# First attention layer: the weighting of the values cut into column halves beside light work, and the transposed maxima moved one step later into another bank ring

## The chip, the cores and the metric

The kernel runs on one core of a Trainium2 chip. The metric is the device time of one execution in microseconds (us); the times of a kernel are given as the median over several runs. Besides these there is one profiled execution, whose instruction records the profile is made of. Engines are named as in the profile: PE is the matrix engine, PEld its weight loads, DVE the vector engine, ACT the scalar engine, POOL the general-purpose engine, SP the one that issues most DMAs.

## The reference, cut to what matters

The model is two layers of attention, each with two attention blocks and a feed-forward block, on x of 2 x 512 rows of 512 numbers. The change is inside the first block, a latent attention with 32 heads, a query latent of 12 and a key latent of 4:

```python
C_q = x @ Wq_d + bq_d
C_kv = x @ Wkv_d + bkv_d
q = (C_q @ W_qk + b_qk).reshape(b, s, NUM_HEADS, KV_LAT)
scores = jnp.einsum('bqhd,bkd->bhqk', q, C_kv) / jnp.sqrt(jnp.asarray(KV_LAT, x.dtype))
attn = jax.nn.softmax(scores, axis=-1)
V = (C_kv @ Wv_u + bv_u).reshape(b, s, NUM_HEADS, HEAD_DIM)
out = jnp.einsum('bhqk,bkhd->bqhd', attn, V).reshape(b, s, NUM_HEADS * HEAD_DIM)
return out @ Wo + bo
```

There is no mask, so every one of 512 queries sees 512 keys. Since the values are an up-projection of a latent of 4, the kernel weights the latent itself (4 numbers and a one, which sums the weights) and applies a folded product of the up-projection and `Wo` afterwards.

## The kernel before

`attn_latent_small` holds all eight PSUM banks. Four heads make a quartet; 32 heads in 2 batches are 16 quartets, called units u = 0 to 15 here. A unit has these operations, each on a tile of 128 by 512:

- `score` (L589, reduce at L597): 16 products of 128 queries by 512 keys, four heads g on four row groups of 32 rows of PE. DVE takes the row maximum of each. The results rotate through a ring of three banks, kind "S" (banks 0 to 2).
- `split` (L606, L607) on POOL, then `maxima` (L615, L199, L618): four PE transposes of the maxima, one correcting product, and an ACT copy into `qm`, the queries with their maxima folded in. Before the change the result lies in an "S" bank.
- `transposed` (L627, L630): the scores again, keys down and queries across, and their exponents by ACT into `pt` or `room`. The results rotate through a ring of three banks, kind "T" (banks 3 to 5).
- `values` (L637): for one key tile, four products with 32 columns of weights each (one for each head, side by side in the columns of PE), over 512 queries, summed in bank 6 over the 4 key tiles and the 4 quartets of a half.

The order of PE is written out by hand; the other engines' order follows from a scheduler. The loop takes eight steps for a unit. Every step issues two scores (of a unit 12 steps ahead), then two transposed scores, which use the two row groups that the two scores leave free. After them an even step issues `values` of a key tile that is two tiles behind, and an odd step a piece of other work (`slices`): a chained product L473, a `head` projection L503 with its ACT copy L513 and its POOL pair L481 and L482, a `divide`, a product L686 or L903, a layer norm's transposes L228, or an `add`, which is a POOL addition L248 and nothing on PE. Step 6 has `maxima` of the next unit between the transposed scores and `values`. The `qm` that it makes is first read by `transposed` in step 0 of the next unit.

So a step is one burst of four row-group products followed by one larger piece, and PE takes its work strictly in this order: a product whose bank is not yet free holds back all that follows. A "S" bank is freed by DVE's reduce, a "T" bank by ACT's exponent (or by the copy to `qm`).

Other engines' orders that matter: DVE runs the reduces of L597 in order with small work of the pieces (L525 and L560 for example), ACT the exponents in order with the copies of the pieces.

Of the kernel before, what the change touches and what calls it, by code (L numbers as in the profile page):

```python
# [38 lines left out]
B, S, D = 2, 512, 512  # L39
P = 128  # L40
NT = S // P
KC = D // P
NTILES = B * NT
# [385 lines left out]
def attn_latent_small(k, a):  # L429
# [9 lines left out]
    with ExitStack() as ctx:  # L439
# [31 lines left out]
        def chained(ps, pairs):  # L471
            for i, (lhsT, rhs) in enumerate(pairs):
                nc.tensor.matmul(ps, lhsT, rhs, start=(i == 0), stop=(i == len(pairs) - 1))  # L473
                yield 1

        def halved(engine, out, full, at, tag="high"):

            top = lp.tile(list(out.shape), F32R, tag=tag, name="high")  # L480
            engine.tensor_scalar(top, full, low[:, at : at + 1], 1.0, ALU.mult, ALU.mult)  # L481
            return engine.tensor_tensor(out, full, top.bitcast(F32), ALU.add).ins  # L482
# [3 lines left out]
        def latents(b):  # L486
            ps = k.turn()
            yield from chained(ps, [(wkvd[:, c], k.xT[b][:, c]) for c in range(KC)])
            full = fulls[b] = one([P, S], "full")
            nc.vector.tensor_scalar(full, ps, bkvc, None, ALU.add)  # L490
            k.latest = halved(nc.gpsimd if b else nc.vector, keys[b], full, 0)

        def queries(b):
            ps = k.turn()
            yield from chained(ps, [(wqd[:, c], k.xT[b][:, c]) for c in range(KC)])
            full = one([P, S], "full")
            nc.vector.tensor_scalar(full, ps, bqd, 0.5, ALU.add, ALU.mult)
            cqs[b] = one([P, S], "cq", F32R)
            halved(nc.gpsimd if b else nc.vector, cqs[b], full, 2)

        def head(b, t):
            ps = k.turn()
            nc.tensor.matmul(ps, wqks[:, t], cqs[b], start=True, stop=True)  # L503
            if (b, t) < (0, 2):
                top = lp.tile([P, S], F32R, tag="high", name="high")
                nc.scalar.copy(top, ps)
                yield 1
                k.correct(ps, rest, top)
                nc.scalar.copy(qs[b][:, t], ps)
                yield 0  # L510
                return
            full = one([P, S], "wv_diag")
            nc.scalar.copy(full, ps)  # L513
            halved(nc.gpsimd, qs[b][:, t], full, 1)
            yield 1

        def latent_values(b):

            tp = k.turn()
            for t in range(NT):  # L520
                nc.tensor.transpose(tp[:, bass.ts(t, P)], fulls[b][:, bass.ts(t, P)], k.ident)
            part = tp.rearrange("p (t d) -> p t d", t=NT)[:, :, 0:5]
            for i in range(4):
                to = vals[b][:, :, i, 5 * i : 5 * i + 5]
                k.latest = nc.vector.tensor_copy(to, part).ins  # L525
            yield 1
# [12 lines left out]
        def fold():  # L539

            wv_diag = one([P, KC, H, 4], "wv_diag")
            nc.vector.tensor_tensor(
                wv_diag,
                own.unsqueeze(3).broadcast_to([P, KC, H, 4]),
                wvT.unsqueeze(2).broadcast_to([P, KC, H, 4]),
                ALU.mult,
            )
            yield 0
            ps = k.turn()
            yield from chained(  # L550
                ps, [(wv_diag[:, c].rearrange("p h d -> p (h d)"), wo[:, c]) for c in range(KC)]
            )
            nc.scalar.copy(folded, ps)
# [3 lines left out]
        def fold_bias():  # L557

            bv_rep = one([P, KC, P], "wv_diag")
            nc.vector.tensor_copy(bv_rep, bvu.unsqueeze(2).broadcast_to([P, KC, P]))  # L560
            yield 0
            ps = k.turn()
            yield from chained(ps, [(bv_rep[:, c], wo[:, c]) for c in range(KC)])
            bias = one([P, D], "bias_all")
            nc.vector.tensor_tensor(bias, ps, bo, ALU.add)
            added.append(bias)

        def add(t):
            with tc.issue_after(k.pooled):
                k.add_bias(t, added[0])  # L570
            yield 1

        quartets = [(b, half, i) for b in range(B) for half in range(2) for i in range(4)]
        last = len(quartets) - 1
        qm, probs, raws, ctxs = {}, {}, {}, {}
# [4 lines left out]
        of_values, other = 6, (7,)  # L580

        def own_bank(kind):
            turns[kind] = (turns[kind] + 1) % 3
            return k.held[:, banks[kind][turns[kind]]]
# [16 lines left out]
        def split(u):  # L601


            every = nm[u % 2].rearrange("p t (g e) -> p t g e", g=4)
            top = lp.tile([P, NT, 4], F32R, tag="top", name="top")
            nc.gpsimd.tensor_copy(top, every[:, :, :, HIGH])  # L606
            k.pooled = nc.gpsimd.tensor_tensor(  # L607
                every[:, :, :, LOW], every[:, :, :, HIGH], top.bitcast(F32), ALU.subtract
            ).ins

        def maxima(u):
            b, half, i = quartets[u]
            tp = own_bank("S")
            for qt in range(NT):
                nc.tensor.transpose(tp[:, bass.ts(qt, P)], nm[u % 2][:, qt], k.ident)  # L615
            k.correct(tp, unit, qs[b][:, 4 * half + i])
            t = lp.tile([P, S], F32R, tag="qm", name="qm")
            nc.scalar.copy(t, tp)  # L618
            qm[u] = t
# [9 lines left out]
            )  # L629
            nc.scalar.activation(probs[u, kc][:, g], ps, AF.Exp)  # L630

        def values(u, kc):
            b, half, i = quartets[u]
            acc = k.held[:, of_values]
            pt = probs.pop((u, kc))
            for g in range(4):
                nc.tensor.matmul(  # L637
                    acc[rows[g]],
                    vals[b][:, kc, i],
                    pt[:, g],  # L640
                    start=(i == 0 and kc == 0),
                    stop=(i == 3 and kc == NT - 1),
                )
            if i == 3 and kc == NT - 1:
                raws[u] = one([P, S], "raw")
                nc.scalar.copy(raws[u], acc)
                extra.extend(following(u))
# [91 lines left out]
        def next_scores():  # L739
            at = next(scores, None)  # L740
            if at:
                u, qt, p = at
                for g in (2 * p, 2 * p + 1):
                    score(u, qt, g)
                if (qt, p) == (NT - 1, 1):
                    split(u)
# [47 lines left out]
        extra = [centre(NT, NT + 1), head(0, 2), head(0, 3), put(NT), put(NT + 1)]  # L794
        extra += [centre(NT + 2, NT + 3), latent_values(0), head(0, 4), put(NT + 2)]
        extra += [put(NT + 3), head(0, 5), head(0, 6), head(0, 7)]

        later = [queries(1), latents(1)] + [head(1, t) for t in range(4)] + [latent_values(1)]
        later += [fold_bias()] + [head(1, t) for t in range(4, 8)] + [fold()]
        later += [add(t) for t in range(NTILES)]  # L800

        behind = []
        with tc.manual_schedule(engines={mybir.EngineType.PE}):
            for n in range(12):
                next_scores()
                slices(1)
                fill(2, of_values)
                if n == 7:
                    with tc.issue_after(k.latest):
                        adapter_coefficients(k, a)  # L810
                if n == 8:
                    maxima(0)
            run(extra)
            extra = later
            k.ring = other
            for u in range(len(quartets)):
                if u == last:
                    k.ring = (0, 1, 2, 7)
                for step in range(8):
                    next_scores()  # L820
                    for g in (2, 3) if step % 2 == 0 else (0, 1):
                        transposed(u, step // 2, g)
                    if step == 6 and u < last:
                        maxima(u + 1)
                    if step % 2 == 0 and len(behind) > 1:
                        values(*behind.pop(0))
                        if u == last:
                            slices(1)
                    else:
                        slices(2 if u == last else 1)  # L830
                    if step % 2:
                        behind.append((u, step // 2))
            k.ring = (0, 1, 2, 3, 4, 5, 7)
            for at in behind:
                values(*at)
            run(extra)
# [1518 lines left out]
```

## Time and profile before

| | us |
|---|---|
| median of 3 runs | 1966.57 (1964.31 to 1967.5) |
| the profiled execution's own time | 1969.02 |
| its span, first to last instruction | 1967.3 |
| the stage of the first attention's 16 units | about 42 to 255 of the span |
| PE busy in the span | 1929.8 (98%) |
| DVE, ACT, POOL busy | 1372.4, 937.8, 1019.7 |

The times of the stage below are read from the timeline (instructions in order of time, one engine at a time) and from busy times of chosen stretches. In a timeline line the first number is the start, the second the length; a run of records is merged, with its count after "x", and what the engine waited for just before stands in brackets. Starts are in us from the start of the span. A matmul in 32-bit floats without the rounded type has two records.

### The profile page before, as it was taken

What the parts mean: (1) busy time and instruction counts of PE and PEld (TensorE: products, weight loads), DVE (VectorE), ACT (ScalarE), POOL (GpSimd) and SP (SyncE); (2) the same over time, 40 slices, a digit from 0 to 9 for tenths busy, and PEclk for the clock granted to TensorE, in tenths of its full rate; (3) what the DMA queues carried; (4) which work ended last, traced back from release to release, by engine and by line L of the source; (5) the groups of instructions that cost most, each with busy time, mean ns of one, the idle gap of its engine ahead of it and who ended that gap; (6) DMA issues with size and microseconds to landing.
All of it is one profiled execution on the core that took longest, in us unless ns stands there. A gap on an engine that the chain in (4) does not pass through costs nothing.

```text
span 1967.3 us, 40475 instructions
## 1 busy us (share of the span) xinstructions
PE 1929.8 (98%) x15610; PEld 1195.7 (61%) x15610; DVE 1372.4 (70%) x3457; ACT 937.8 (48%) x2460; POOL 1019.7 (52%) x1112
## 2 busy tenths in 40 slices
PE   9989999999999999999999999999999999999999
PEld 5333356777777777777777545666566554654554
DVE  8889658767776676777765577777677755847853
ACT  3876624444444343444443267666666411641550
POOL 4331055776756667677763246565655545216221
PEclk9999999999999999999999999999999999999999
DMA  3010222322321322232222213020101002002001
GB/s 136 17 44 1 75 68 65 90 73 88 98 65 50 97 76 81 76 98 76 79 79 85 71 22 109 7 74 7 62 13 55 25 9 49 2 2 43 2 2 43
DMA packets 69296, 108.96 MB, mean 55 GB/s; under 512 B 13922, under 2 KB 48994, under 8 KB 62052
## 3 DMA queue, kind: packets, MB, share of 16 engines
q1 hardware_dynamic: 68804, 104.15, 18.2%
q8 instruction: 127, 2.08, 0.4%
q0 software_dynamic: 288, 2.10, 0.3%
q14 instruction: 77, 0.63, 0.1%
HBM read 80.00 MB, written 4.19 MB: 43 GB/s over the span
## 4 chain that ended last, share of the span: by engine, by line
PE 87%; DVE 5%; POOL 5%; issue 1%; ACT 1%; DMA 0%; SPq 0%; DVEq 0%; POOLq 0%
PE held L1004 13%; PE held L281 11%; PE held L1139 9%; PE held L190 9%; PE held L357 8%; PE held L637 3%; PE held L589 3%; PE held L1076 3%; PE held L473 2%; PE sc L190 2%; PE held L1498 2%; PE held L1495 1%; PE pj L190 1%; PE tp L1771 1%; PE held L1496 1%
## 5 line engine op out<-in xcount | busy, mean ns | idle before, releaser
L302 ACT ACTIVATE room<-room,nmax 128x128 f32<-128x128 f32 (+3 forms) x384 | 212.6, 557 | 354.4 <-DVE nmax L292 352.0
L281 PE MATMUL held<-kT,q 128*32 128x32 f32 (+15 forms) x4096 | 264.2, 397 | 5.3 <-DVE invs L310 1.7
L292 DVE CUSTOM_DVE_ANT_0 room<-held,mask 128x128 f32<-128x128 f32 (+3 forms) x384 | 179.1, 488 | 62.5 <-PE held L281 57.0
L281 PEld LDWEIGHTS held<-kT,q 128*32 128x32 f32 x4096 | 143.4, 110 | 87.2 <-issue 37.7
L357 PE MATMUL held<-turned,vals 32*128 32x384 f32 (+7 forms) x2784 | 189.7, 416 | 0.9 <-issue 0.9
L597 DVE TENSOR_REDUCE nm<-held 128x1 f32<-128x512 f32 x256 | 161.7, 684 | 23.4 <-PE held L627 14.6
L357 PEld LDWEIGHTS held<-turned,vals 32*128 32x128 f32 (+1 forms) x2784 | 149.3, 167 | 39.8 <-issue 23.2
L315 ACT ACTIVATE room<-room,invs 128x128 f32<-128x128 f32 (+3 forms) x316 | 153.3, 551 | 41.8 <-DVE invs L310 41.7
L254 DVE TENSOR_TENSOR rows<-rows,held 128x512 f32<-128x512 f32 x198 | 129.5, 673 | 31.9 <-PE held L1004 31.3
L330 DVE STREAM_TRANSPOSE turned<-room 128x1152 f32<-128x1152 f32 x80 | 107.9, 1361 | 41.2 <-ACT room L315 21.6
L243 POOL TENSOR_TENSOR rstd<-ve,mhalf 128x1 f32<-128x1 f32 x64 | 36.2, 569 | 179.5 <-DVE ve L241 176.3
L1165 POOL TENSOR_TENSOR q<-q,room 128x256 f32<-128x256 f32 x64 | 45.3, 729 | 123.4 <-DVE q L1148 112.8
L1183 POOL TENSOR_TENSOR q<-q,cosq 128x512 f32<-128x512 f32 x60 | 88.0, 1467 | 31.6 <-DVE t L1180 31.6
L1139 PE MATMUL held<-room,w 128*128 128x256 f32 x384 | 95.0, 383 | 0.0
L1184 POOL TENSOR_TENSOR q<-q,t 128x512 f32<-128x512 f32 x64 | 86.8, 1356 | 6.3 <-DVE q L1183 2.5
L302 ACT ACTIVATE probs<-probs,nmax 128x128 f32<-128x128 f32 (+3 forms) x128 | 70.6, 553 | 37.8 <-DVE nmax L292 37.0
L589 PEld LDWEIGHTS held<-keys,qs 32*128 32x128 f32 x256 | 30.9, 181 | 94.2 <-DVE nm L597 67.5
L1004 PE MATMUL held<-w,ctxT 128*128 128x256 f32 x360 | 86.5, 383 | 0.1
L630 ACT ACTIVATE pt<-held 128x512 f32<-128x512 f32 x128 | 69.7, 598 | 29.8 <-PE held L627 24.9
L630 ACT ACTIVATE room<-held 128x512 f32<-128x512 f32 x128 | 69.8, 599 | 26.7 <-PE held L627 25.0
L589 PE MATMUL held<-keys,qs 32*128 32x512 f32 x256 | 76.9, 494 | 5.5 <-DVE nm L597 5.1
L2105 POOL TENSOR_SCALAR_AFFINE_SELECT room<-room 128x512 f32<-128x512 f32 x32 | 20.3, 635 | 118.0 <-ACT room L2101 118.0
(439 smaller groups left out, 5011.0 us busy)
## 6 DMA issues: line engine op xcount, KB each, us to landing
w<-in_b_wq SPq DMA_DIRECT2D x16, 1024.0 KB, 4.8
w<-in_b_wo SPq DMA_DIRECT2D x16, 1024.0 KB, 5.2
vals<-v SPq DMA_DIRECT2D x256, 64.0 KB, 2.1
w<-in_m_wo SPq DMA_DIRECT2D x8, 1024.0 KB, 6.7
w<-in_b_wk SPq DMA_DIRECT2D x16, 256.0 KB, 2.8
w<-in_b_wupv SPq DMA_DIRECT2D x16, 256.0 KB, 2.6
w<-in_m_wqn SPq DMA_DIRECT2D x8, 384.0 KB, 3.4
rows<-in_x SPq DMA_DIRECT2D x8, 256.0 KB, 4.7
```

The costliest lines, as they stand in the source:

```text
L190: last = self.nc.tensor.matmul(out, lhsT, rhs, start=(i == 0), stop=(i == len(pairs) - 1))
L254: self.nc.vector.tensor_tensor(x, x, ps.rearrange("p (t d) -> p t d", t=2), op)
L281: nc.tensor.matmul(ps[32 * i : 32 * i + 32, a - lo : b - lo], q[:, at : at + 32], keys[:, a:b], start=True, stop=True,)
L292: nc.vector.tensor_tensor_reduce(out=row, in0=ps[:, :kv], in1=self.mask_back[:, :kv] if qt % 2 else self.mask[:, S - kv :], op0=ALU.add, o ...
L302: nc.scalar.activation(row, row, AF.Exp, bias=nmax, scale=-1.0, accum_out=total[:, qt : qt + 1])
L315: self.nc.scalar.activation(row, row, AF.Identity, scale=each)
L357: self.nc.tensor.matmul(out[:, :, :n], values(i, j), rhs, start=(j == blocks[0]), stop=(j == stop[i]),)
L589: nc.tensor.matmul(ps, qs[b][rows[g], 4 * half + i, bass.ts(qt, P)], keys[b][rows[g]], start=True, stop=True,)
L597: k.latest = nc.vector.tensor_reduce(nm[u % 2][:, qt, at : at + 1], ps, AX.X, ALU.max, negate=True).ins
L630: nc.scalar.activation(probs[u, kc][:, g], ps, AF.Exp)
L1004: k.nc.tensor.matmul(out, lhsT[:, i, bass.ts(t, P)], rhs[i], start=not (after or t or i), stop=i == 1, skip_group_check=True,)
L1139: nc.tensor.matmul(out, lhsT[:, c], rhs[:, c], start=c == 0, stop=c == 1)
```

## The change

It does two things, both in the order of PE.

- `maxima` of the next unit moves from step 6, where it stood behind the transposed scores, to step 7, where it stands between the two scores and the two transposed scores; and it takes its bank from the "T" ring instead of the "S" ring.
- `values` can be told to do a part of the columns. Where the next piece of other work is a `head` or an `add`, or there is none, a step 0, 2 or 4 issues only columns 0 to 255 of the four products, and the next odd step issues columns 256 to 511 ahead of its piece. The first and last tile of a sum are excepted. Laid out, this happens for 10 tiles: three of unit 2 (steps 0, 2, 4), one of unit 4 (step 0) and three each of units 6 and 7; 80 matmuls of 256 columns stand where 40 of 512 stood.

ACT, POOL and SP keep their orders. DVE's order differs in a few places: in unit 2 the copy L560 goes ahead of the copies L525 and of the reduces of step 6, in unit 4 the multiplication L542 goes behind the reduces of step 7, and in one place of the second batch two layer-norm operations change places with two reduces.

```diff
         def maxima(u):
             b, half, i = quartets[u]
-            tp = own_bank("S")
+            tp = own_bank("T")
...
-        def values(u, kc):
+        def values(u, kc, lo=0, hi=S):
             b, half, i = quartets[u]
-            acc = k.held[:, of_values]
-            pt = probs.pop((u, kc))
+            acc = k.held[:, of_values, lo:hi]
+            pt = probs[u, kc]
             for g in range(4):
                 nc.tensor.matmul(
                     acc[rows[g]],
                     vals[b][:, kc, i],
-                    pt[:, g],
+                    pt[:, g, lo:hi],
                     start=(i == 0 and kc == 0),
                     stop=(i == 3 and kc == NT - 1),
                 )
+            if hi < S:
+                return
+            probs.pop((u, kc))
+            acc = k.held[:, of_values]
...
                 for step in range(8):
                     next_scores()
+                    if step == 7 and u < last:
+                        maxima(u + 1)
                     for g in (2, 3) if step % 2 == 0 else (0, 1):
                         transposed(u, step // 2, g)
-                    if step == 6 and u < last:
-                        maxima(u + 1)
+                    if second:
+                        values(*second.pop(), S // 2, S)
                     if step % 2 == 0 and len(behind) > 1:
-                        values(*behind.pop(0))
+                        at = behind.pop(0)
+                        light = not extra or extra[0] in heads + adds
+                        ends = (quartets[at[0]][2], at[1]) in ((0, 0), (3, NT - 1))
+                        if light and step < 6 and not ends:
+                            values(*at, 0, S // 2)
+                            second.append(at)
+                        else:
+                            values(*at)
```

More of the change, by code (lines that the diff above doesn't have):

```diff
@@ L796, in attn_latent_small @@
         extra += [put(NT + 3), head(0, 5), head(0, 6), head(0, 7)]
[L798 to L802, printed above, removed]
+        heads = [head(1, t) for t in range(8)]
+        adds = [add(t) for t in range(NTILES)]
+        later = [queries(1), latents(1), *heads[:4], latent_values(1)]
+        later += [fold_bias(), *heads[4:], fold(), *adds]
+        behind, second = [], []
         with tc.manual_schedule(engines={mybir.EngineType.PE}):
```

## The prediction

> **What bounds the kernel now.** I read the page's busy times and its chain first, to see which engine's order sets the end. PE is busy 98% of the span, and most of the chain is PE's own.
>
> ```profile
> PE 1929.8 (98%) x15610; PEld 1195.7 (61%) x15610; DVE 1372.4 (70%) x3457; ACT 937.8 (48%) x2460; POOL 1019.7 (52%) x1112
> PE 87%; DVE 5%; POOL 5%; issue 1%; ACT 1%; DMA 0%; SPq 0%; DVEq 0%; POOLq 0%
> ```
>
> That is an average over the whole span; the change touches only 42 to 255 us. So next I asked for the busy times of the stretches of this stage (first column: the stretch and its length, then PE, PEld, DVE, ACT).
>
> ```profile
> 42.00:62.00 20.00, 20.00 (x115) 6.57 (x113) 17.40 (x29) 14.35 (x27) 5.28 (x9) 1.00 0.05 15
> 118.00:144.00 26.00, 22.15 (x158) 7.88 (x155) 22.15 (x38) 20.00 (x38) 8.23 (x10) 1.00 0.02 7
> 176.00:212.00 36.00, 35.82 (x224) 13.85 (x227) 30.67 (x54) 24.87 (x48) 6.16 (x11) 1.00 0.22 74
> ```
>
> There are two regimes. Where the odd steps carry a chained product (42 to 62, 176 to 235) PE has no gap: "heavy". In units 6 and 7 (118 to 144), where they carry only an `add`, PE idles 3.85 of 26 us: "light". The timeline shows both. Steps 6 and 7 of unit 0, heavy:
>
> ```profile
> 51.47 0.50 PE L589 MATMUL held<-keys,qs 32*128 32x512 f32 x2
> 51.91 0.66 PE L615 MATMUL held<-ident,nm 128*128 128x128 f32 x4
> 52.32 0.47 PE L199 MATMUL held<-qs,unit 128*128 128x512 f32 x1
> 52.72 1.07 PE L637 MATMUL held<-pt,vals 128*32 128x512 f32 x8
> 53.72 0.50 PE L589 MATMUL held<-keys,qs 32*128 32x512 f32 x2
> 54.15 1.12 PE L473 MATMUL held<-room,w 128*128 128x512 f32 x2
> ```
>
> Starts give the prices, since records overlap: a burst of two scores and two transposed scores 0.43 (53.72 to 54.15), `maxima` 0.81 (51.91 to 52.72), `values` 1.00, a chained product 1.05. Step 6 of unit 6, light, on PE and then DVE:
>
> ```profile
> 125.74 0.50 PE L589 MATMUL held<-keys,qs 32*128 32x512 f32 x1 [0.41 <-DVE nm L597]
> 126.43 0.63 PE L615 MATMUL held<-ident,nm 128*128 128x128 f32 x4 [0.18 <-DVE nm L597]
> 128.22 0.50 PE L589 MATMUL held<-keys,qs 32*128 32x512 f32 x2
> ...
> 125.00 2.48 DVE L597 TENSOR_REDUCE nm<-held 128x1 f32<-128x512 f32 x4 [0.21 <-PE held L627]
> 128.75 2.48 DVE L597 TENSOR_REDUCE nm<-held 128x1 f32<-128x512 f32 x4 [1.27 <-PE held L589]
> ```
>
> Here PE waits for DVE to free a bank, and a little later DVE runs dry: `maxima` holds one of three "S" banks, and PE spends 1.8 us on `maxima` and `values` before the next scores. DVE idles 1.27 once and about 0.22 three times in a unit, 1.93 in all, of the 11.87 from `maxima` at 126.43 to the next at 138.30.
>
> Two more readings price what the trace of before does not have: row-group products in twos, and `values` of half the columns.
>
> ```profile
> 37.85 0.49 PE L589 MATMUL held<-keys,qs 32*128 32x512 f32 x2
> 38.27 0.50 PE L503 MATMUL held<-cq,wqks 128*128 128x512 f32 x1
> ...
> 230.20 0.50 PE L627 MATMUL held<-qm,keys 32*128 32x512 f32 x2
> 230.63 1.06 PE L637 MATMUL held<-room,vals 128*32 128x512 f32 x8
> ...
> L281 PE MATMUL held<-kT,q 128*32 128x512 f32 x256 | 131.7, 596 | 2.2 <-ACT ctxT L372 1.3 <-DVE invs L310 0.9
> L281 PE MATMUL held<-kT,q 128*32 128x256 f32 x256 | 76.6, 381 | 0.0
> ```
>
> Two scores alone take 0.42 and two transposed alone 0.43, as long as all four together. The last two lines (groups with shapes apart; mean ns behind the busy time) are matmuls of the shape of `values`: 596 ns for 512 columns, 381 for 256.
>
> Last, ACT in unit 2, whose odd steps carry a `head`:
>
> ```profile
> 71.17 2.27 ACT L630 ACTIVATE pt<-held 128x512 f32<-128x512 f32 x4
> 73.45 0.59 ACT L513 COPY wv_diag<-held 128x512 f32<-128x512 f32 x1
> 73.94 2.20 ACT L630 ACTIVATE room<-held 128x512 f32<-128x512 f32 x4
> ```
>
> Four exponents and a copy follow without a gap: 2.77 for two steps (71.17 to 73.94), where two steps of PE last 2.70 (`values` to `values`, 68.06 to 70.76). Head units are bound by ACT as well, so cheaper PE or DVE time gains nothing there.
>
> **Maxima between scores and transposed scores.** Its five PE matmuls per unit are the same 0.81. But the burst of step 7 is cut in two of 0.42 each: +0.42 on PE, 15 times at most. What of it shows depends on the unit.
>
> Heavy, no cover: units 0, 10, 11 and 13, 4 x 0.42 = +1.7. In 10 and 11 DVE has work of its own, but it waits there for L903, which itself moves back.
>
> Behind `maxima` wait, on PE, all that follows, and on ACT the copy to `qm`, now ahead of step 7's exponents. With t the end of L199, `qm` is ready at t + 0.69 (0.10 to its start, 0.59 long) and the first exponent of step 7 ends at t + 1.24. Its bank is the one that the second transposed score of the next step 0 needs. PE gets there at t + 0.43 plus the piece: after a product at t + 1.48, no wait; after a `head` at t + 0.85, 0.4 late; after an `add` at t + 0.43, 0.8 late. This is the new stall, in the "T" ring, in place of the old one in the "S" ring.
>
> Units 1 and 2, followed by hand from 63.53: PE reaches step 0 of unit 2 no later than before, but ACT starts the exponents of step 7 about 0.2 later and stays the bound, each `transposed` waiting for it. Step 6 of unit 2 is late by 0.67. There L560, now ahead of L525 and the reduces in DVE's queue, waits for POOL's L482 (end 76.18 before) and puts the reduces back by about 0.5. Step 7's piece ends at 80.45 in place of 79.69: +0.76. This holds the three splits of unit 2, which by ACT's 2.77 gain nothing.
>
> Unit 3 (a `head` in step 7): PE +0.42, and ACT's continuous row 92.76 to 102 starts that much later: +0.45. Unit 4: its step 7 waits 0.94 for DVE's L542, itself waiting on the POOL pair behind a `head`; the 0.42 goes into that: 0. Its one split lies beside that ACT row: 0. Unit 5: step 0 came late for a DVE wait of 0.56, and now comes late for the "T" ring, 118.48 against 118.06 with a shift of 0.43 already in it: 0. Unit 9: DVE is busy without a gap from 157 to 176 and has a backlog when step 7 comes: 0. Unit 12: a wait of 0.18 on the "S" ring goes, 0.42 and a short "T" wait come: +0.25. Unit 14 issues no scores in step 7: 0.
>
> **Values in halves.** The difference 596 - 381 = 215 ns, for two passes one after the other, makes a half 1.00 - 0.43 = 0.57: 1.14 for both, +0.14 of PE for each of 10 splits. In units 6 and 7 PE has 3.85 us to spare, so that is hidden. A light step then costs PE 0.43 + 0.57 = 1.00, and DVE 2 x 0.62 = 1.24 (2.48 for four): DVE should run through steps 1 to 5. What remains idle is about 0.4 before the reduces of step 0 and 0.6 after them (from the "T" stall). A unit is 16 x 0.62 + 1.0 = 10.95 against 11.87: -0.9, twice: -1.8. Unit 8 starts with DVE further ahead, and the PE waits of 0.43 in its steps 2 and 6 shrink: -0.4.
>
> The Trainium skill, page "TensorEngine Tiling (Array Packing)", section "Instruction Overhead", gives each matmul about 60 cycles of overhead; at 2.4 GHz that would make two halves cost 1.05, by my estimate, in place of 1.14, and the sum would be the same, as both are hidden. The same page, "Key Properties", says that changing the tiling mode drains the engine, which speaks against this change: step 7 and each split add mode changes. The 0.42 rows hold such a drain already, so nothing is added for it.
>
> **Sum:** 1.7 + 0.76 + 0.45 + 0.25 - 1.8 - 0.4 = +0.96 us. The other engines' work and all DMAs stay in their order, and what follows 255 us is shifted. Against the profiled run (1969.02, span 1967.3) that is a span of about 1968.3; that run is 2.5 above the median of 1966.57, so the median should be 1967.6.
>
> Bounds of what the trace does not show. The cut burst: from 0 (the scores overlap with the transposes of the maxima) to 0.42 in all 14 units that issue scores there, 5.9; I take the unit-by-unit sum above, 3.2. A light unit: from no gain (the "T" stall takes it all) to DVE's whole idle time, -1.93; I take -0.9, which is near half. A split in a head unit: from -0.22 (one DVE gap) to +0.14 (its PE price); I take 0.
>
> **The rivals.**
> *The "T" ring takes the place of the "S" ring (slower).* Its place is step 0 after each `maxima`, its price the 0.8 of the light units, with the gain of units 6 to 8 gone, and 0.42 in 14 units: +5.9, 1972.5. It decides if ACT is not free at t, that is if the exponents of step 6 end after L199. For it: ACT is continuous in units 2 and 4, and the two transposed scores behind `maxima` wait on no other engine than ACT. Against it: in units 6 and 7 ACT is busy 20.0 of 26 us and rests 0.9 behind the copy to `qm`.
> *DVE runs without a gap (faster).* Units 6 and 7 gain 1.93 each, unit 5 its 0.96 of DVE idle time behind `maxima`, unit 8 the gaps of 0.22 and 0.87, less the certain 1.7 of the heavy units: -4.2, 1962.4. For it: the gaps are all laid to PE. Against it: the stall of t + 1.24 lies in the same place.
> *Nothing happens:* the cut burst overlaps after all and ACT holds the light units too: 1966.6, within the range of the first.
>
> **How the numbers follow.** About 0.2%, 3.9 us, is what a measurement of this kernel can tell from no change. My forecast, with gains and losses of 2 to 3 us each that nearly cancel, has a chance of 0.54, with its own range of 1964.5 to 1970; nothing happens, 0.08; slower by the "T" ring, or by part of it, 0.24; faster, 0.14. So faster 0.14, same 0.62, slower 0.24. The range goes from the faster rival to a little past the slower one, 1962.2 to 1973.
>
> **What would show it.** Right: in unit 0, L615 starts 0.43 behind L589 of step 7 and L627 0.81 behind that, with no gap, and the unit is 0.42 longer; `values` x8 of 256 columns start 0.57 before what follows; from one `maxima` to the next in units 6 and 7 it is about 11 us, with ACT named as what the second transposed score of step 0 waited for; DVE's 1.27 gaps are gone. Wrong: if L627 of step 7 starts less than 0.8 behind L615; if heavy units keep their length; if light units keep 11.87; or if anything behind 255 us changes its length by more than a microsecond, of which I have no account.

## The result, and the profile after

The changed kernel takes 1970.32 us in the median of 22 runs (1966.59 to 1974.75), the kernel before 1967.39 in the median of 22 runs taken beside it: a ratio of 1.0017, with an interval from 1.0011 to 1.0024. The forecast was 1967.6, its range 1962.2 to 1973.0. So the change makes the kernel slower by about 2.9 us, which is under the 0.2% named in the prediction, and in the forecast's direction, but about three times its +0.96. Four runs were far longer for no reason that the kernels show, two of the kernel before (3829 and 4847 us) and one each of e2 and e4 below (6617 and 4167); they count in the medians but not in ratios and means, and without them the kernel before has a median of 1967.14.

The profiled execution of the changed kernel took 1971.35 us (span 1969.6). The page's busy times and the head of its chain:

```profile
PE 1936.5 (98%) x15690; PEld 1200.3 (61%) x15690; DVE 1372.8 (70%) x3457; ACT 937.4 (48%) x2460; POOL 1022.7 (52%) x1112
PE 88%; POOL 5%; DVE 5%; issue 1%; ACT 1%; DMA 0%; SPq 0%; DVEq 0%; POOLq 0%; ACTq 0%
```

PE is busy 6.7 us longer than before, with 80 matmuls more. That number can't be read as work: two products that run side by side count once, and twice when the second has to wait until the first is done, and a product under a lower clock counts for longer (both are seen below). For the same reason a table of waits answers little here. What answers is the length of each unit, from the first `values` of its step 0 to that of the next (timeline of PE):

| unit | before | after | change | forecast |
|---|---|---|---|---|
| opening: burst of step 0 of unit 0 to that of step 2 | 3.15 | 3.92 (see below) | +0.77 | none made |
| 0, from its step 2 | 10.28 | 10.71 | +0.43 | +0.42 |
| 1, 2 | 24.49 | 25.42 | +0.93 | +0.76 |
| 3 | 12.30 | 12.82 | +0.52 | +0.45 |
| 4 | 13.34 | 13.40 | +0.06 | 0 |
| 5 | 12.29 | 12.67 | +0.38 | 0 |
| 6, 7 | 23.74 | 21.98 | -1.76 | -1.8 |
| 8 | 12.71 | 12.60 | -0.11 | -0.4 |
| 9 | 13.60 | 13.87 | +0.27 | 0 |
| 10, 11, 13 | 42.58 | 43.71 | +1.13 | +1.28 |
| 12 | 13.66 | 13.80 | +0.14 | +0.25 |
| 14 | 12.91 | 12.83 | -0.08 | 0 |
| sum | | | +2.68 | +0.96 |

The heavy units first. Steps 6 and 7 of unit 0 on PE, after:

```profile
53.89 0.50 PE L589 MATMUL held<-keys,qs 32*128 32x512 f32 x2
53.90 0.49 PE L627 MATMUL held<-qm,keys 32*128 32x512 f32 x2
54.32 1.07 PE L637 MATMUL held<-pt,vals 128*32 128x512 f32 x8
55.32 0.50 PE L589 MATMUL held<-keys,qs 32*128 32x512 f32 x2
55.75 0.66 PE L615 MATMUL held<-ident,nm 128*128 128x128 f32 x4
56.16 0.47 PE L199 MATMUL held<-qs,unit 128*128 128x512 f32 x1
56.56 0.49 PE L627 MATMUL held<-qm,keys 32*128 32x512 f32 x2
56.98 1.13 PE L473 MATMUL held<-room,w 128*128 128x512 f32 x2
```

The uncut burst of step 6 costs 0.43 (53.89 to 54.32). In step 7 the two scores alone cost 0.43 (55.32 to 55.75) and the two transposed scores alone 0.42 (56.56 to 56.98). There is no gap. This is the cut burst as it was priced.

A light unit, from step 5 of unit 6 to the first steps of unit 7, PE:

```profile
128.67 0.64 PE L637 MATMUL held<-room,vals 128*32 128x256 f32 x8
129.24 0.67 PE L589 MATMUL held<-keys,qs 32*128 32x512 f32 x2
...
130.86 0.50 PE L589 MATMUL held<-keys,qs 32*128 32x512 f32 x2
131.29 0.66 PE L615 MATMUL held<-ident,nm 128*128 128x128 f32 x4
131.70 0.47 PE L199 MATMUL held<-qs,unit 128*128 128x512 f32 x1
132.11 0.50 PE L627 MATMUL held<-qm,keys 32*128 32x512 f32 x2
132.44 0.39 PE L589 MATMUL held<-keys,qs 32*128 32x512 f32 x2
132.85 0.99 PE L627 MATMUL held<-qm,keys 32*128 32x512 f32 x2
133.78 0.64 PE L637 MATMUL held<-room,vals 128*32 128x256 f32 x8
```

And DVE and ACT in the same stretch:

```profile
123.89 7.26 DVE L597 TENSOR_REDUCE nm<-held 128x1 f32<-128x512 f32 x12 [0.72 <-PE held L627]
131.39 1.29 DVE L597 TENSOR_REDUCE nm<-held 128x1 f32<-128x512 f32 x2 [0.23 <-PE held L589]
132.87 1.29 DVE L597 TENSOR_REDUCE nm<-held 128x1 f32<-128x512 f32 x2 [0.19 <-PE held L589]
...
129.99 1.09 ACT L630 ACTIVATE pt<-held 128x512 f32<-128x512 f32 x2
132.21 0.59 ACT L618 CAST qm<-held 128x512 fp32r<-128x512 f32 x1 [1.14 <-PE held L199]
132.70 1.09 ACT L630 ACTIVATE pt<-held 128x512 f32<-128x512 f32 x2
```

DVE now runs twelve reduces in a row (before, four between gaps), and idles 1.14 in a unit instead of 1.93; a half of `values` costs 0.57 (128.67 to 129.24). The new stall stands where it was forecast, but nothing in brackets tells of it. The two transposed scores of step 0 start 0.41 behind the scores instead of with them, when `qm` is there (132.21 and 0.59), and they no longer run side by side: their row is 0.99 long instead of 0.50, and `values` starts 0.93 behind them instead of 0.43. The second one alone, on PE, and the first exponent of step 7 alone, on ACT:

```profile
133.35 0.50 PE L627 MATMUL held<-qm,keys 32*128 32x512 f32 x1
132.70 0.60 ACT L630 ACTIVATE pt<-held 128x512 f32<-128x512 f32 x1
```

The second transposed score starts 0.05 after that exponent ends. ACT takes `qm` first, at 132.21, and only then the exponents of step 7, whose banks step 0 needs.

The opening is the part that the prediction lacks. Here is first the timeline of PE before, then after:

```profile
42.21 0.66 PE L589 MATMUL held<-keys,qs 32*128 32x512 f32 x2
42.38 0.50 PE L627 MATMUL held<-qm,keys 32*128 32x512 f32 x2
42.81 1.12 PE L473 MATMUL held<-room,w 128*128 128x512 f32 x2
```

```profile
42.26 0.67 PE L589 MATMUL held<-keys,qs 32*128 32x512 f32 x2
42.44 0.49 PE L627 MATMUL held<-qm,keys 32*128 32x512 f32 x1
43.22 0.49 PE L627 MATMUL held<-qm,keys 32*128 32x512 f32 x1 [0.29 <-ACT wv_diag L513]
43.64 1.93 PE L473 MATMUL held<-room,w 128*128 128x512 f32 x2
```

The two transposed scores of step 0 of unit 0 no longer start together: the second waits for ACT's copy of a `head`, and starts 0.78 later. The first `maxima(0)`, issued once ahead of the loop, takes its bank through the same line as all others. There it turns the ring of "T" by one against the pieces of the opening, which use banks of the same ring, and step 0 meets the bank of a `head` that ACT has not yet copied. In this profiled execution the product behind it also ran under a lower clock (1.93 long instead of 1.12), which has nothing to do with the change and is taken up at the end; the 3.92 in the table is that of an experiment (e3) with the same opening and without the lower clock; two more (e1 and e4) give 3.91 and 3.93. In the profile of the changed kernel itself it is 5.51 (42.26 to 47.77).

### The profile page after: what moved, and what is told of

Read it like the earlier page. It is cut to its first block, busy times and chain, and to the rows that moved or that the text cites. A ratio compares the mean times of both kernels' runs of the same rounds, so it can differ in the third digit from the quotient of the medians.

```text
span 1969.6 us, 40617 instructions
## 1 busy us (share of the span) xinstructions
PE 1936.5 (98%) x15690; PEld 1200.3 (61%) x15690; DVE 1372.8 (70%) x3457; ACT 937.4 (48%) x2460; POOL 1022.7 (52%) x1112
## 4 chain that ended last, share of the span: by engine, by line
PE 88%; POOL 5%; DVE 5%; issue 1%; ACT 1%; DMA 0%; SPq 0%; DVEq 0%; POOLq 0%; ACTq 0%
PE held L1018 13%; PE held L281 11%; PE held L1153 9%; PE held L190 9%; PE held L357 8%; PE held L637 3%; PE held L589 3%; PE held L1090 3%; PE held L473 2%; PE sc L190 2%; PE held L1512 2%; PE held L1509 1%; PE pj L190 1%; PE tp L1785 1%; PE held L1510 1%; PE sc L2105 1%
## 5 line engine op out<-in xcount | busy, mean ns | idle before, releaser
L589 PEld LDWEIGHTS held<-keys,qs 32*128 32x128 f32 x256 | 30.2, 182 | 84.7 <-DVE nm L597 53.8
L1533 POOL TENSOR_TENSOR q<-t,t 64x512 f32<-64x512 f32 x62 | 79.1, 1276 | 4.9
L1153 PEld LDWEIGHTS held<-room,w 128*128 128x128 f32 x384 | 71.4, 190 | 14.4 <-issue 2.0
```

The costliest lines, as they stand in the source:

```text
L589: nc.tensor.matmul(ps, qs[b][rows[g], 4 * half + i, bass.ts(qt, P)], keys[b][rows[g]], start=True, stop=True,)
L1153: nc.tensor.matmul(out, lhsT[:, c], rhs[:, c], start=c == 0, stop=c == 1)
```

## The experiments

The time of a run moves by several us with PE's granted clock (last section), so the main reading is the length of five stretches of the profiled execution: the opening, units 0 to 5 (from step 2 of unit 0), units 6 and 7 (light), units 8 to 13, and unit 14. The last column of the table is a check from all runs: the mean time of each kernel, put to a clock of 1 with the slope of the last section, against the same for the kernel before, as it ran beside the experiments.

| kernel | opening | 0-5 | 6-7 | 8-13 | 14 | sum against before | median us (runs) | at clock 1, against before |
|---|---|---|---|---|---|---|---|---|
| before | 3.15 | 72.70 | 23.74 | 82.55 | 12.91 | | 1967.39 (22) | |
| the change | 3.92 | 75.02 | 21.98 | 83.98 | 12.83 | +2.7 | 1970.32 (22) | +2.7 |
| e1 maxima alone | 3.91 | 75.00 | 24.05 | 83.97 | 12.85 | +4.7 | 1972.35 (6) | +4.9 |
| e2, e8 halves alone | 3.14 | 72.95 | 21.84 | 82.52 | 12.90 | -1.7 | 1966.00 (11) | -1.6 |
| e3 behind | 3.92 | 72.50 | 21.42 | 81.51 | 12.61 | -3.1 | 1963.47 (10) | -2.8 |
| e4 step 6, "T" bank | 3.93 | 72.47 | 21.15 | 81.91 | 12.91 | -2.7 | 1965.43 (11) | -2.0 |
| e5 behind, first in "S" | 3.14 | 72.44 | 21.41 | 81.45 | 12.60 | -4.0 | 1963.13 (11) | -4.2 |
| e6 change, first in "S" | 3.15 | 74.95 | 21.99 | 83.92 | 12.85 | +1.8 | 1969.48 (11) | +1.5 |
| e7 cut, "S" bank | 3.14 | 75.61 | 21.95 | 84.93 | 12.83 | +3.4 | 1967.72 (1) | +3.3 |
| e9 combined | 3.15 | 73.63 | 21.24 | 81.57 | 12.61 | -2.9 | 1965.22 (11) | -2.5 |
| e10 behind, no halves | 3.14 | 73.63 | 23.57 | 81.47 | 12.62 | -0.6 | 1965.47 (10) | -0.6 |

The sums and the last column agree within 0.4 us but for e4 (0.7), which stays open. By the ratio of the times alone, e3 (0.9995, 0.9985 to 1.0004), e4 (0.9992, 0.9983 to 1.0002) and e10 (0.9992, 0.9983 to 1.0001) can't be told from the kernel before; there the stretches decide. e2 and e8 are the same kernel: its stretches are those of e8, its median that of e2.

My theory after the result: the cut burst is the cost, and the halves are the gain. The rivals: the stall comes from the "T" bank itself; the gain of the light units comes from where `maxima` stands.

### The two halves of the change apart

e1 keeps the move of `maxima` and issues all `values` whole:

```diff
-                        light = not extra or extra[0] in heads + adds
+                        light = False
```

> Only the first half of the change: the maxima move, no tile of the values is cut. Three stretches of PE's timeline are compared with the kernel before: units 0 to 5 (burst of step 2 of unit 0 to the first values of unit 6: 72.70 before, 75.02 with the whole change), units 6 and 7 (first values of unit 6 to those of unit 8: 23.74 and 21.98), units 8 to 13 (first values of unit 8 to those of unit 14: 82.55 and 83.98). My theory (the cut burst costs 0.42 in heavy units, only the halves pay back in light ones): units 0 to 5 75.0, units 6 and 7 24.1 (no gain, +0.2 per unit for the stall on the T ring), units 8 to 13 84.0; +4.1 in all, about 1971.5. Rival (the move itself frees the S ring and is what the light units gain by): units 6 and 7 stay near 22.0, +1.9 in all.

Measured 75.00, 24.05 and 83.97: the theory's numbers. Against before, 1.0032 with an interval from 1.0020 to 1.0044. The move by itself makes light units slower by 0.31, so their gain is not from it.

e2 keeps the halves and puts `maxima` back into step 6 and an "S" bank:

```diff
-            tp = own_bank("T")
+            tp = own_bank("S")
...
-                    if step == 7 and u < last:
-                        maxima(u + 1)
                     for g in (2, 3) if step % 2 == 0 else (0, 1):
                         transposed(u, step // 2, g)
+                    if step == 6 and u < last:
+                        maxima(u + 1)
```

> Only the second half: the same 10 tiles in halves, the maxima in step 6 in the S ring as before. My theory: units 0 to 5 72.7 (head units are bound by ACT, so the halves of units 2 and 4 give nothing), units 6 and 7 22.4 (three pairs of steps each 0.22 shorter, the 1.27 gap of DVE stays), units 8 to 13 82.5; -1.3 in all, about 1966. Rival (the halves cost their 0.14 each on PE): units 6 and 7 at 24.6, +1.4 in all.

The times give 0.9996 (0.9986 to 1.0005). The stretches come from a further run of the same kernel:

> The halves alone once more, for a profile: opening 3.15, units 0 to 5 72.7, units 6 and 7 22.4, units 8 to 13 82.5 by my theory; by the rival (halves cost on PE) units 6 and 7 24.6.

Measured 72.95, 21.84 and 82.52. The rival fell: the halves alone take 1.90 from the light units, 0.6 more than the theory's 1.3, with the stall of step 6 still there. DVE in a light unit of e8:

```profile
128.63 9.65 DVE L597 TENSOR_REDUCE nm<-held 128x1 f32<-128x512 f32 x16 [1.26 <-PE held L627]
```

It still idles 1.26 behind `maxima`, but then runs all sixteen reduces of a unit in a row. With the change a unit's idle time is 1.14: there the move only swaps one stall for another of nearly the same length, and all of the light units' gain is from the halves. In heavy units they do nothing, since none stands there, and in units 0 to 5 they cost 0.25 with `maxima` in step 6, 0.22 of it in unit 2.

### The cut burst

e3 leaves `maxima` in step 7 and in the "T" ring, but issues it behind the transposed scores, so that the burst of four is whole:

```diff
-                    if step == 7 and u < last:
-                        maxima(u + 1)
                     for g in (2, 3) if step % 2 == 0 else (0, 1):
                         transposed(u, step // 2, g)
+                    if step == 7 and u < last:
+                        maxima(u + 1)
```

> The whole change, but with the maxima of step 7 behind the two transposed scores, so that the burst of four is not cut; still one step later and in the T ring. My theory (the cut is the cost in heavy units): units 8 to 13 82.8, units 0 to 5 73.5 (the lateness of ACT in units 1 to 3 remains in part), units 6 and 7 21.4 (step 0 waits for the copy to qm alone); -1.3 in all. Rival (being one step later is the cost, through the wait for qm and ACT): units 8 to 13 stay at 84.0 and units 0 to 5 at 75.0.

Measured 72.50, 21.42 and 81.51: beside heavy work more than the theory's gain, and the rival fell. Units 0 to 5 and 8 to 13 are each 2.5 shorter than with the change, and the latter 1.04 shorter than before. Kernels e5 and e6, below, show the same pair without the longer opening.

e4 goes back to step 6, with the bank from the "T" ring, and halves only beside adds, there for all four tiles:

```diff
-                    if step == 7 and u < last:
-                        maxima(u + 1)
                     for g in (2, 3) if step % 2 == 0 else (0, 1):
                         transposed(u, step // 2, g)
+                    if step == 6 and u < last:
+                        maxima(u + 1)
...
-                        light = not extra or extra[0] in heads + adds
+                        light = not extra or extra[0] in adds
...
-                        if light and step < 6 and not ends:
+                        if light and not ends:
```

> What the theory says should beat both: the maxima stay in step 6 behind the transposed scores, but in the T ring; halves only beside an add (units 6 and 7), there for all four tiles of a unit. No burst is cut, qm has a whole step to get ready, and no S bank is taken. My theory: units 0 to 5 72.5, units 6 and 7 20.8 (DVE idle only about 0.4 per unit), units 8 to 13 82.3; -3.4 in all, about 1964. Rival (the T ring is the dearer place for the maxima wherever it is, since ACT must empty it): units 0 to 5 and 8 to 13 each longer than before by 0.5 or more, and units 6 and 7 not under 21.5.

Measured 72.47, 21.15 and 81.91. The rival fell, since none of its three stretches is longer than before; the light units keep 0.35 more than the theory's 20.8. Where no halves stand, in units 8 to 13, the "T" bank alone is worth 0.6 (82.52 in e8 to 81.91), and the later step another 0.4 (81.51 in e3).

### The first maxima

Both e3 and the change have the longer opening. e5 is e3, and e6 is the change, each with the one `maxima` ahead of the loop back in an "S" bank:

```diff
-        def maxima(u):
+        def maxima(u, bank="T"):
...
-            tp = own_bank("T")
+            tp = own_bank(bank)
...
-                    maxima(0)
+                    maxima(0, "S")
```

> The version with the maxima of step 7 behind the transposed scores, and the very first maxima (before unit 0) back in an S bank. A fourth stretch, the opening, runs from the burst of step 0 of unit 0 to that of step 2: 3.15 before, 3.92 in every version run so far with the first maxima in a T bank, where the second transposed score of unit 0 waits 0.29 for ACT's L513. Theory (the first maxima turn the T ring by one against the opening pieces, which use the same banks 3 to 5, so that score meets a bank that a head still holds): opening 3.15, units 0 to 5 72.5, units 6 and 7 21.4, units 8 to 13 81.5: -3.9 in the stage, about 1963. Rival (the 0.77 comes from something else in the opening): opening stays 3.92, -3.1.

> The change as it is, but the first maxima in an S bank. Theory: opening 3.15 in place of 3.92, the other stretches as with the change (75.0, 22.0, 84.0): +1.9 against the kernel before, where the whole change is +2.7. Rival: opening 3.92, +2.7.

Both came as expected: the opening is 3.14 and 3.15, all else is unchanged. So the opening's 0.77 is that one bank. e5 is faster than both kernels: 0.9980 of the time before, with an interval from 0.9971 to 0.9989. e6 is 1.0012 (1.0003 to 1.0021).

The two differ only in whether `maxima` stands behind the transposed scores of step 7 or ahead of them. Ahead, it cuts the burst on PE, and on ACT it puts the copy to `qm` in front of the exponents; no run does one without the other. Their stretches differ by 2.51, 0.58, 2.47 and 0.25: 5.8 us in all, and no unit is without its share (from 0.19 in unit 10 to 0.85 in unit 2). Unit 14 has its 0.25 without a cut, since its step 7 issues no scores. Step 7 and the next burst in a light unit of e5, PE and then ACT:

```profile
126.26 0.50 PE L589 MATMUL held<-keys,qs 32*128 32x512 f32 x2
126.27 0.50 PE L627 MATMUL held<-qm,keys 32*128 32x512 f32 x2
126.70 0.66 PE L615 MATMUL held<-ident,nm 128*128 128x128 f32 x4
127.11 0.47 PE L199 MATMUL held<-qs,unit 128*128 128x512 f32 x1
127.52 0.52 PE L589 MATMUL held<-keys,qs 32*128 32x512 f32 x2
128.48 0.50 PE L627 MATMUL held<-qm,keys 32*128 32x512 f32 x2 [0.44 <-ACT qm L618]
128.91 0.64 PE L637 MATMUL held<-room,vals 128*32 128x256 f32 x8
...
126.86 1.08 ACT L630 ACTIVATE pt<-held 128x512 f32<-128x512 f32 x2 [0.39 <-PE held L627]
127.84 0.59 ACT L618 CAST qm<-held 128x512 fp32r<-128x512 f32 x1
```

The scores of step 7 and its transposed scores start together and cost 0.44. ACT has its exponents done before `qm`. There is a wait here too, for `qm` itself, and from the scores of step 7 to the next `values` it is 2.65 us; with the change it is 2.92 (130.86 to 133.78). Of this, the burst of step 0 takes 1.39 here (127.52 to 128.91) and 1.34 with the change (132.44 to 133.78): with the other order the stall in step 0 has another cause and the same length. What `maxima` ahead costs a light unit is 0.28; the heavy units 0, 11 and 13 pay 0.52 to 0.61, units 1, 8, 10 and 12 only 0.19 to 0.30.

### The bank or the order of ACT

e7 is the change with `maxima` in the "S" ring, the burst cut as in the change:

```diff
-            tp = own_bank("T")
+            tp = own_bank("S")
```

> The change with the maxima in step 7, cutting the burst, but in the S ring. Theory (the stall of step 0 comes from ACT, which has the copy to qm ahead of the exponents of step 7, and not from the bank that the maxima take): opening 3.15, units 0 to 5 75.0, units 6 and 7 22.0 or more, units 8 to 13 84.0. Rival (my prediction's word of a T ring in place of the S ring: the bank that the maxima take is what the second transposed score of step 0 misses): units 6 and 7 about 21.0, units 0 to 5 about 74.

Measured 75.61, 21.95 and 84.93. The light units are as with the change (21.98), so the stall in step 0 is not from the "T" bank that `maxima` takes. It stays when that bank is not taken, and the second transposed score starts at 131.40, again 0.05 after the first exponent of step 7 ends, as it would if ACT's order is the cause. Units 0 to 5 and 8 to 13 are worse by 0.6 and 1.0: there `maxima` waits for DVE again, as before the change (timeline of PE in unit 8 of e7):

```profile
153.18 0.63 PE L615 MATMUL held<-ident,nm 128*128 128x128 f32 x4 [0.20 <-DVE nm L597]
```

Units 2, 3, 8, 9, 10 and 11 each have such a wait of about 0.2 and are longer than with the change by 0.21 to 0.24.

### What e5 gains, and from which part

e9 is e5 with halves only beside adds, there for all four tiles; e10 is e5 with no halves. Against e5:

```diff
-                        light = not extra or extra[0] in heads + adds
+                        light = not extra or extra[0] in adds
...
-                        if light and step < 6 and not ends:
+                        if light and not ends:
```

```diff
-                        light = not extra or extra[0] in heads + adds
+                        light = False
```

> The kernel with the maxima behind the transposed scores of step 7 and the first ones in an 'S' bank (stretches 3.14 / 72.44 / 21.41 / 81.45 / 12.60), with the halves only beside adds, there for all four tiles of a unit. Theory (halves gain where DVE runs dry, and nothing beside a head): opening 3.14, units 0 to 5 72.4, units 6 and 7 21.15 as in the kernel with step 6 and all four halves, units 8 to 13 81.5; about 0.3 us less than that kernel, 1962.9 in the median, which the timing can't tell from it. Rival (the fourth half, now beside the maxima in step 7, holds back the product of the maxima's copy): units 6 and 7 21.7 or more.

> The same placing of the maxima (behind the transposed scores of step 7, 'T' bank, the first in an 'S' bank), and no halves. Theory (the gain of the light units comes from the halves, the heavy units' from the place and the bank): units 0 to 5 72.5, units 6 and 7 23.2 (21.41 and the 1.9 that the halves alone gained), units 8 to 13 81.5; 1965. Rival (the uncut later place alone takes away the wait of step 6): units 6 and 7 22.0 or less, 1963.7.

In the light units both theories held: 21.24 with all four tiles in halves (the rival wanted 21.7 or more), 23.57 with none (23.2 against 22.0). The halves are worth 1.90, 2.07 and 2.16 us there, in three places of `maxima` (before to e8, e1 to the change, e10 to e5).

In units 0 to 5 both expectations failed: 73.63 in both, instead of 72.4 and 72.5. Against e5, 0.9 of this is in unit 2, which is 12.84 and 12.83 long instead of 11.94, and nearly all of the rest in unit 4 (13.35 and 13.33 instead of 13.08), which I have not followed. No halves stand in unit 2 of these two kernels, and the order that the scheduler gives DVE is another. Unit 2 of e10, PE and DVE:

```profile
78.19 0.47 PE L199 MATMUL held<-qs,unit 128*128 128x512 f32 x1
79.46 1.12 PE L473 MATMUL held<-w,wv_diag 128*128 128x512 f32 x2 [0.81 <-DVE wv_diag L560]
...
76.60 2.47 DVE L597 TENSOR_REDUCE nm<-held 128x1 f32<-128x512 f32 x4
79.00 0.41 DVE L560 COPY wv_diag<-a_bvu 128x512 f32<-128x512 f32 x1
```

And DVE of e5 in the same place:

```profile
76.19 0.42 DVE L560 COPY wv_diag<-a_bvu 128x512 f32<-128x512 f32 x1
76.53 0.43 DVE L525 COPY vals<-held 128x20 f32<-128x20 f32 x4
76.87 2.50 DVE L597 TENSOR_REDUCE nm<-held 128x1 f32<-128x512 f32 x4
```

The copy L560, operand of the next product, stands behind four reduces in e10 and ahead of them in e5; PE's L473 waits 0.81 for it. So the halves of unit 2 are worth 0.9 in e5, and not for PE's sake. e9 is thus slower than e5 in the sum of its stretches (0.9986, 0.9977 to 0.9995, against before), and e5 stays the best.

The change can now be put together from before, step by step, by the sums of the table: `maxima` behind step 7 in the "T" ring, -0.6 (e10); the halves, -3.4 (to e5), of which -2.2 in the light units; `maxima` ahead of the transposed scores, which cuts the burst, +5.8 (to e6); the first `maxima` in the "T" ring, +0.9. That is the +2.7 of the result: the third step alone takes back more than the first two gain. How its 5.8 divides into the cut on PE and the order on ACT isn't shown; 0.43 of PE time is seen in the cut itself.

## Why the prediction was right or wrong

**Heavy, no cover: right,** but for unit 10. Four times 0.42 was 1.7; units 0, 10, 11 and 13 gave 0.43, 0.18, 0.49 and 0.46, 1.56 together. What covers unit 10 I have not followed.

**Units 1 and 2: the size right, the way not.** +0.93 against +0.76. The wait of L560 for POOL, which I had followed by hand and which was to put the reduces back by 0.5, costs nothing: L560 starts at 79.33, when L482 has just ended (79.28) and DVE has only then done the reduces ahead of it. In unit 2 the way from `values` of step 0 to those of step 6 takes 8.61, against 9.15 before less the 0.81 of `maxima`, +0.27; from there to the next unit's it takes 4.21, against 2.92 and the 0.81, +0.48, which is about the cut. A wait that goes with L560 does exist, of PE's L473 for it, but in the kernels without halves there: 0.81 in e10, 0.40 in e1.

**Units 3 and 4: right,** +0.52 and +0.06.

**Unit 5: wrong.** "118.48 against 118.06 with a shift of 0.43 already in it: 0" took the cut of this very unit for a shift that came from outside. The unit is 0.38 longer.

**Units 6 and 7: right,** -1.76 against -1.8, with units of 10.99 against "about 11". (16 x 0.62 + 1.0 is 10.92, not 10.95; measured are 9.84 of reduces and 1.14 idle.) The stall of the "T" ring was put at t + 1.24 for the first exponent's end; that end is at 133.30, t + 1.13 (t = 132.17), and `values` stands at t + 1.61, where t + 1.24 + 0.43 would be 1.67. That the second transposed score waits for this exponent is read from the trace, and e7 rules out the bank that `maxima` takes. What I did not see is that the move has no part in the gain: the halves alone give -1.90 (e8).

**Units 8, 9 and 12: sizes off.** -0.11, +0.27 and +0.14 against -0.4, 0 and +0.25. In unit 8 the reason was wrong too, DVE further ahead by the halves: with the halves alone it keeps its length (12.71 in e8), without any and with `maxima` behind in the "T" ring it is 0.39 shorter (12.32 in e10), and `maxima` ahead takes 0.26 of that back (e5 to e6). The cover that I named for the cut in unit 9, DVE's backlog, was not enough: e6 and e5 differ by 0.55 there. What ends last in step 7 of unit 9 I have not followed further.

**What the sum lacks: the opening, +0.77.** I read the step "maxima takes its bank from the T ring" in the loop, and not for the call ahead of it. With unit 5 (0.38), unit 8 (0.29) and unit 9 (0.27) this makes 1.71, all of the difference between +0.96 and +2.68; the other rows cancel. Another 0.8 up to the measured median is the base: the prediction counted from 1966.57, the median of 3 runs (with +0.96 that is 1967.5, not 1967.6), and 22 runs give 1967.39. So the forecast of a small loss came true by a sum of gains and losses that nearly cancel, and its nearness is in part luck.

**Values in halves: right as priced** (0.57 each, 1.14 for two). The estimate of 1.05 for two halves, from the page "TensorEngine Tiling (Array Packing)" of the Trainium skill, is under the measurement, which decides. A split in a head unit, put at 0 between -0.22 and +0.14, is 0 with the change (units 2 and 4 are 12.82 and 13.40 long, in e1 12.82 and 13.37). But the three splits of unit 2 together range from -0.9 (e10 to e5) to +0.22 (before to e8). The upper end is within the bound of three times 0.14; the lower is beyond three times -0.22, because the halves also change where the scheduler puts DVE's small copies.

**The rivals.** Slower by the "T" ring: its price had two parts, and only one is there. The full cut, 5.8 us between e5 and e6, is nearly its 5.9, though not in 14 equal parts (0.19 to 0.85), but the placing and the halves pay back more than half; and the light units keep their gain, against this rival. DVE without a gap did not come: 1.14 of its 1.93 idle time stays. Nothing happens fell with the 0.42 of unit 0.

**What would show it.** L615 starts 0.43 behind L589 and L627 0.81 behind that; both held. ACT as the named reason of the stall did not: PE has no gap there, since the first transposed score still runs while the second waits. From 237 or 242 us, the first `values` of the last unit, to the end of the span it is 1730.0 before and 1728.0 after, a change of more than a microsecond, of which I had no account then. Here the lower clock lies in other places of the two profiles, three behind 255 us before and one after (last section). By the last column of the table, at equal clock, the stage and its opening hold all of the change's 2.7, and nothing is left behind them.

## What to carry to other kernels

A burst of products that share the array is one price: here two of four cost as much as all four (0.42 to 0.43), so a piece that would stand in between is tried behind the burst (e5 against e6, 5.8 us over 15 units). When an operation changes its ring of banks, every call is walked through, the single one ahead of a loop too, and the first use of the ring behind it (0.77 here). When a hand-written order of one engine is edited, the order that a scheduler derives for the others is compared operand by operand: one small copy behind four reduces cost 0.8 us on PE.

## What the runs showed of the hardware

PE's granted clock falls to half (0.50) for 3.4 us at a time, in some executions and not in others. The profile of the kernel before has three such dips, at 1160.3, 1747.3 and 1808.8 us, that of the changed kernel two, at 43.8 and 1811.9; those of e3, e5 and e7 have none until the last 4 us of the span, where every profile has the lower clock. Over all eleven profiles (e2's is left out) there are fourteen dips, at four places: near 1160 in five profiles, near 1810 in six, near 1746 in two and at 43.8 in one. The busy times of three stretches of the changed kernel, and then of two of the kernel before (columns: stretch, length, busy time of PE, PEld, DVE, ACT and POOL, granted clock of PE, share of DMA, GB/s):

```profile
39.00:43.60 4.60, 4.17 (x15) 1.87 (x13) 4.60 (x12) 1.60 (x3) 3.08 (x4) 1.00 0.00 0
43.60:47.00 3.40, 3.40 (x8) 1.16 (x8) 1.24 (x3) 1.27 (x4) 1.63 (x2) 0.53 0.00 0
1745.00:1751.00 6.00, 5.92 (x56) 3.13 (x48) 0.00 (x0) 3.74 (x9) 1.12 (x2) 1.00 0.01 3
```

```profile
1162.00:1166.00 4.00, 4.00 (x19) 1.42 (x12) 2.67 (x12) 3.28 (x13) 3.85 (x5) 0.79 0.26 55
1745.00:1751.00 6.00, 6.00 (x35) 2.95 (x38) 0.68 (x2) 4.08 (x14) 2.54 (x4) 0.72 0.00 0
```

In the first, PE was busy 4.17 of the 4.60 us ahead and all through the dip. The dip stretches the opening of the changed kernel from the 3.92 of e3 to 5.51. Since PE is the bound, such dips set most of the scatter: over 172 runs of these kernels, each against its own mean, the time rises by 1.5 us for each 0.001 that the mean clock falls, and the seven runs of the kernel before with a clock of 1.000 lie within 0.5 us (1963.90 to 1964.42), while the others of that kernel reach 1970.7. That is as large as the change, so a single profiled execution can mislead by it: the spans shown differ by 2.3 us, since the kernel before had more of its dips in the profile than the changed one.

The Trainium skill, page "TensorE: Matmul & The Clock Gate", section "What's actually happening", lets the clock fall to half after an idle window of about 3.4 us. The length and the ratio of the dips agree with it. The cause does not as it stands: in the 3.41 us ahead of a dip PE was never idle throughout. It was busy for 1.37 to 2.47 us of them near 1160 and 1810, which may point that way, but for 3.33 near 1746 and 2.98 at 43.8. What sets the dips off stays open; no run here was made for it.
